# Two 16-head attentions on one core: steps taken in pairs, values gathered in bursts, projections in 32-column tiles

## The chip, the core and the metric

The kernel runs on one core of a Trainium2 chip. The core has a matrix engine (TensorE, PE in the profile, with its weight loads listed as PEld), a vector engine (DVE), a scalar engine (ACT), a general-purpose engine (POOL) and a queue that starts transfers (SP). PE reads its operands from the on-chip memory SBUF and writes results to the accumulation memory PSUM, which has 8 banks of 2 KB per partition; here a bank holds a 128 x 512 float32 tile. ACT and DVE read PSUM, POOL does not.

The metric is the device time of one execution in microseconds (us). Three runs of the kernel before took 1714.59, 1716.47 and 1717.76 us; the median is 1716.47.

## The reference

The input x is 8 batches of 512 tokens of 128 numbers. Four blocks follow each other, each of the form x = layernorm(x + block(x)):

1. attention with 16 heads of 8 numbers and a bias that falls with the distance of key and query (ALiBi);
2. a gated feed-forward whose operands are rounded to a 4-bit float grid in blocks of 16;
3. the same attention without the bias;
4. two layers of a windowed attention with 8 heads of 64 and a gated feed-forward.

The change concerns blocks 1 and 3 (called attention 1 and attention 2 here):

```python
qkv = (x @ W_qkv.T + b_qkv).reshape(B, S, 3, 16, 8)         # q, k, v: [B, 16, S, 8]
scores = einsum('bhqd,bhkd->bhqk', q, k) / sqrt(8)           # S = 512
probs = softmax(scores - slope[h] * |pos_q - pos_k|)         # the bias in attention 1 only
out = einsum('bhqk,bhkd->bhqd', probs, v) -> [B, S, 128]
y = out @ W_out.T + b_out
```

## The kernel before, in words

All work is float32, or float32 read in a mode that PE passes through once ("fp32r"). A plain float32 product is issued as two PE instructions, which is why the profile counts twice the products that the code names.

**Units and steps.** An attention runs over 32 units: 8 batches times 4 groups of 4 heads. The 4 heads of a unit are two pairs (`pp` = 0, 1); the two heads of a pair (`j` = 0, 1) lie in partitions 0 to 63 and 64 to 127 of the operands `q` and `k`, so that two products with half the rows of the array run at once. A unit has 8 steps in each of two passes, and the second pass of a unit runs 16 steps (`LAG`) after the first, beside the first pass of the unit two further on. One call of `step` does one step of both:

- first pass, called S below: two products write the scores of 128 queries against 512 keys into `s_ps` (two banks, of which there are two sets, pool `as`); DVE takes the maximum over the keys (`m`, a TENSOR_REDUCE from 128 x 1024);
- second pass, called T below: two products write the scores transposed, 128 keys against 512 queries, into two banks `t_ps`. One row of `q` holds minus the maximum, so these scores are already shifted. In attention 1 four small products (called C below, `corrected`) add the part of the bias inside a block. ACT takes the exponentials into two tiles `e` (pool of 11).

On PE the order of a step is S, T, C. On ACT it is exp, exp. After the step come the functions that are listed for it in `todo`.

**Values.** `values(u, blk, part)` adds one block of 128 keys for 256 of the 512 queries: 4 products, one for each head of the unit, with 32 output columns each (8 value columns, a column of ones for the denominator, the rest zero). They go to 4 column tiles of the array at once and accumulate in `av`, one PSUM bank of its own (pool `aav`). There is one such call in each step, so PE changes from the half-row tiling of S, T and C to the 32-column tiling and back in each step. After the eighth call ACT copies `av` to `avs` (128 x 512).

**Around it.** `divide` turns `avs` on PE (`o_ps`), and DVE divides by the denominators. `shift` turns the maxima on PE (`m_ps`), ACT copies them, POOL starts two transfers that put them into the row of `q`. Once a batch there are `begin_x` (turn x), `begin_qk` for n = 0 and 1, `begin_v`, `end_o` and `end_y`: each is a product or a turn on PE into a bank and a copy on ACT, or for `end_y` a sum and statistics on DVE. `begin_qk` hands its result on to POOL, which splits it in two parts, and to transfers through DRAM that lay out the operands (`load_qk`). The projections use the whole 128 x 128 array.

**Banks.** PSUM is divided into `as` (2 sets of 2 banks), `at` (3 banks in turn, for T and for every other use) and `aav` (1 bank). A tile that takes a bank waits until the last reader of the tile before it in this bank is done.

**Order.** PE, ACT, DVE and POOL instructions of these stages are held in program order, engine by engine; what sets the order is thus the order of the calls in the loop over steps and the step at which `later` lists a function. `plan` lists them: with z the step at which the second pass of the unit begins, values at z+3 to z+10, `divide` at z+12, `end_o` at z+15, `end_y` at z+18, and the work for a later batch at fixed steps of the batch.

**The other stages.** `ffn0` (block 2) lies between the attentions and uses the same banks; the first pass of attention 2 begins at its end. `ffn1` (block 4) follows; its weights `w1_s` and `w2_s` are loaded during attention 1 into SBUF that is held for the whole kernel.

In the profile, products of the attentions carry line 259, turns line 260, and ACT, DVE and POOL work of the attentions line 48 (the helper that keeps the program order). Line 644 is the same for `ffn1`, 472 for `ffn0`.

Of the kernel before, what the change touches and what calls it, by code (L numbers as in the profile page):

```python
# [18 lines left out]
P = 128  # L19
# [32 lines left out]
def body(ctx, tc, x, consts, rows, wa0, wa1, acols, bo, wf, wqkv, wo, w1, w2, cols, b2r, qs, ks, out):  # L52
# [16 lines left out]
    w1_s = outer.tile([P, 2, 2 * HID], F32, name="w1_s")  # L69
    w2_s = outer.tile([P, 2, 3, D], F32, name="w2_s")  # L70
# [36 lines left out]
    def load_weights():  # L107
        held(out=cst[:, C_MASK0:C_ROT], in_=consts[:, C_MASK0:C_ROT])
        held(out=wa[1], in_=wa1)
        held(out=wqkv_s, in_=wqkv.rearrange("l p f -> p l f"))  # L110
        held(out=wo_s, in_=wo.rearrange("l (c p) d -> p l c d", p=P))
        held(out=w1_s, in_=w1.rearrange("l p f -> p l f"))
        held(out=w2_s, in_=w2.rearrange("l (c p) d -> p l c d", p=P))
        held(out=cols_s, in_=cols)
# [87 lines left out]

    def operand_steps(li, qs_, ks_, va, mm, tr, bank, work, dram, qb):
# [9 lines left out]
        def begin_qk(b, h, n, start=nc.sync.dma_start):  # L213
            ps = bank("qk_ps")
            mm(ps, lhsT=w[:, n * P : (n + 1) * P], rhs=h["xT"], start=True, stop=True)
            t = work.tile([P, S], F32, tag=f"x{n}", name="x", bufs=1)
# [27 lines left out]
        def begin_v(b, h):  # L244
            ps = bank("v_ps").rearrange("p (c d) -> p c d", c=NT)
            for c in range(NT):
                mm(ps[:, c, :], lhsT=h["xT"][:, c * P : (c + 1) * P], rhs=w[:, W_V : W_V + P], start=True, stop=True)
# [5 lines left out]
    def attention(li, alibi, qs_, ks_, va, batch, late=None, spare=None, alone=0):  # L253
# [7 lines left out]
        with ExitStack() as st:  # L261
            pool = lambda name, bufs, **k: st.enter_context(tc.tile_pool(name=f"{name}{li}", bufs=bufs, **k))
            bank = lambda name: p_t.tile([P, S], F32, tag="t", name=name)
# [21 lines left out]
            def step(u, i, v, k):  # L285


                if u:
                    blk, pp = i // 2, i % 2
                    p, lo = 2 * u["g"] + pp, (i // 2) * P  # L290
                    q, kk = qs_[u["b"] % 2], ks_[u["b"] % 2]
                    both = p_s.tile([P, 2, S], F32, tag="s", name="s_ps")
                    ps = [both[:, j, :] for j in range(2)]
                    for j in range(2):
                        r = slice(64 * j, 64 * j + 63)
                        mm(
                            ps[j], lhsT=q[r, p, lo : lo + P], rhs=kk[r, p, :], start=True, stop=True,
                            skip_group_check=True,
                        )
                if v:  # L300
                    vp, vlo = 2 * v["g"] + k % 2, (k // 2) * P
                    q, kk = qs_[v["b"] % 2], ks_[v["b"] % 2]
                    ts = [bank("t_ps") for j in range(2)]
                    for j in range(2):
                        r = slice(64 * j, 64 * j + 64)
                        mm(
                            ts[j], lhsT=kk[r, vp, vlo : vlo + P], rhs=q[r, vp, :], start=True, stop=not alibi,
                            skip_group_check=True,
                        )
                if u:  # L310
                    if i == 0:
                        u["m"] = small.tile([P, 2, 2, NT], F32, tag="m", name="m")
                    dve.tensor_reduce(u["m"][:, :, pp, blk], both, AX.X, ALU.max)
                if v:
                    if alibi:
                        corrected(ts, vlo)
                    for j in range(2):
                        e = work.tile([P, S], F32, tag="e", name="e", bufs=11)
                        act_.activation(e, ts[j], AF.Exp, scale=float(SLOPES[2 * vp + j]) if alibi else 1.0)
                        v["e"].append(e)  # L320

            def shift(u):

                ps = bank("m_ps")[0:16, 0:P]
# [11 lines left out]
            def values(u, blk, part):  # L336
# [982 lines left out]
```

## Time and profile before

The profiled execution took 1715.33 us, of which the profile's span is 1713.6 us. The table gives what matters from the page and from stretches of the span; the granted clock of PE is 1.00 in the two attention stretches.

| stretch | span, us | PE busy | DVE busy | ACT busy |
|---|---|---|---|---|
| whole span | 1713.6 | 1601.4 | 1382.6 | 1257.3 |
| one batch of attention 1 | 53.3 (189.9 to 243.2) | 51.88 | 44.90 | 40.63 |
| one batch of attention 2 | 50.1 (733.3 to 783.4) | 49.24 | 42.87 | 39.90 |

The first S starts at 30 us, T of attention 1 runs from 54 to 472 us, T of attention 2 from 607 to 1005 us; `ffn1` fills the rest.

How to read it: a line of the timeline gives the start, the time from the first start to the last end, the engine, the line of the code, the operation with output and inputs, and how many instructions were merged; in brackets the idle time of the engine ahead of it and what ended that. The time of one product includes some 0.17 us in which the next ones already run, so the distance from start to start is what a product costs PE.

### The profile page before, as it was taken

To read this page: it belongs to the slowest core of one execution; us is meant where nothing else is said; L and a number is where in the kernel's file an instruction comes from. 1 tells how busy PE (TensorE), PEld (TensorE's weight loads), DVE (VectorE), ACT (ScalarE), POOL (GpSimd) and SP (SyncE) were. 2 spreads that over 40 slices of the span, in tenths; PEclk is the share of its full clock that TensorE was granted. 3 is DMA by queue.
4 is the path that set the end of the run, shared out by engine and by line. 5 is a ranking of instruction groups with operands and counts; after the bars stand their busy time and mean duration, and the time that the engine had idled before them with its cause. 6 is when DMAs were issued, how large, how long until landed. Compare 5 with 4: busy or idle time off the path is not lost.

```text
span 1713.6 us, 40048 instructions
## 1 busy us (share of the span) xinstructions
PE 1601.4 (93%) x15281; PEld 932.7 (54%) x15281; DVE 1382.6 (81%) x2220; ACT 1257.3 (73%) x2996; POOL 912.6 (53%) x974
## 2 busy tenths in 40 slices
PE   3999999999988799999999989999999999999995
PEld 1455555555556534444444446666666666666664
DVE  4788888889568888888888748888888888888863
ACT  0577777777745577787787757778888878888883
POOL 3323333232247732223232268888888888888872
PEclk7899999999999989999999989999999999999998
DMA  6626232230010352333231101111111111111110
GB/s 134 154 67 154 54 74 53 57 69 11 8 13 1 80 116 46 73 63 70 59 73 28 45 7 42 35 35 35 41 36 38 38 36 37 44 41 41 36 35 25
DMA packets 92801, 90.11 MB, mean 53 GB/s; under 512 B 45969, under 2 KB 58257, under 8 KB 92610
## 3 DMA queue, kind: packets, MB, share of 16 engines
q1 hardware_dynamic: 87280, 85.49, 23.2%
q8 instruction: 122, 2.00, 0.5%
q10 hardware_dynamic: 1234, 1.52, 0.3%
q0 software_dynamic: 4096, 0.54, 0.2%
q14 instruction: 69, 0.57, 0.1%
HBM read 41.82 MB, written 18.87 MB: 35 GB/s over the span
## 4 chain that ended last, share of the span: by engine, by line
PE 74%; DVE 10%; ACT 6%; POOL 4%; issue 3%; DMA 2%; SPq 0%; DVEq 0%; ACTq 0%; POOLq 0%
PE av L259 15%; PE s_ps L259 11%; PE t_ps L259 8%; PE y_ps L644 5%; PE sp L644 5%; PE o_ps L644 3%; PE t_ps L644 3%; PE v_ps L644 3%; PE p_ps L644 2%; ACT e L48 2%; PE q_ps L644 2%; PE k_ps L644 2%; PE gp L644 2%; DVE m L48 2%; PE ap L644 2%
## 5 line engine op out<-in xcount | busy, mean ns | idle before, releaser
L48 DVE TENSOR_REDUCE m<-s_ps 128x2 f32<-128x1024 f32 x512 | 618.7, 1223 | 124.9 <-PE s_ps L259 116.0
L48 ACT ACTIVATE e<-t_ps 128x512 f32<-128x512 f32 x1024 | 556.7, 597 | 149.8 <-PE t_ps L259 140.7
L259 PE MATMUL av<-e,va 128*32 128x256 f32 x4096 | 328.1, 393 | 14.0 <-ACT avs L48 14.0
L259 PE MATMUL s_ps<-k,q 63*128 63x512 f32 x1024 | 263.4, 509 | 25.0 <-DMA q<-far 16.9
L48 POOL DMA_DIRECT2D q<-mt x128 | 69.1, 544 | 342.9 <-ACT mt L48 342.9
L259 PE MATMUL t_ps<-q,k 64*128 64x512 f32 x1024 | 231.8, 410 | 1.4 <-ACT e L48 1.3
L644 ACT ACTIVATE pw<-sp,m,was_v 128x128 f32<-128x128 f32 x512 | 227.6, 479 | 1.5 <-DVE m L644 1.0
L259 PEld LDWEIGHTS s_ps<-k,q 63*128 63x128 f32 x1024 | 98.7, 188 | 235.1 <-issue 139.7
L644 POOL TENSOR_TENSOR was_v<-was_v 128x16 f32<-128x16 f32 x64 | 187.7, 2933 | 5.3
L259 PEld LDWEIGHTS t_ps<-q,k 64*128 64x128 f32 x1024 | 140.7, 187 | 29.2 <-ACT e L48 16.7
L259 PEld LDWEIGHTS av<-e,va 128*32 128x32 f32 x4096 | 81.5, 108 | 103.8 <-issue 58.9
L644 POOL TENSOR_TENSOR pw<-pw,den 128x1024 f32<-128x1024 f32 x64 | 121.3, 1895 | 9.3 <-DVE den L644 9.3
L644 ACT ACTIVATION_READ_ACCUMULATOR pw<-sp,m,was_v 128x1 f32 x512 | 115.6, 226 | 0.0
L644 DVE TENSOR_REDUCE m<-sp 128x4 f32<-128x512 f32 x128 | 82.2, 683 | 21.8 <-PE sp L644 20.1
L644 POOL TENSOR_TENSOR was_k<-was_k,was_q 128x512 f32<-128x512 f32 x64 | 88.0, 1376 | 6.1 <-DVE was_q L644 6.1
L644 ACT COPY v<-v_ps 128x512 f32<-128x512 f32 x64 | 37.8, 591 | 72.6 <-PE v_ps L644 72.6
L48 POOL CAST parts<-x 128x512 fp32r<-128x512 f32 x32 | 19.5, 609 | 131.0 <-ACT x L48 131.0
L644 PEld LDWEIGHTS t_ps<-cst,was_k 128*128 128x128 f32 x512 | 59.8, 142 | 43.1 <-issue 22.8
L644 DVE COPY pT<-p_ps 128x512 f32<-128x512 f32 x128 | 79.9, 665 | 0.5 <-PE p_ps L644 0.5
L644 PEld LDWEIGHTS p_ps<-cst,pw 128*128 128x128 f32 x512 | 59.8, 141 | 32.3 <-issue 27.5
L644 DVE TENSOR_REDUCE was_v<-was_k 128x16 f32<-128x1024 f32 x64 | 77.1, 1204 | 0.0
L644 PE MATMUL y_ps<-wo_s,oT 128*128 128x128 f32 x512 | 73.9, 288 | 0.0
(191 smaller groups left out, 3189.9 us busy)
## 6 DMA issues: line engine op xcount, KB each, us to landing
far<-parts SPq DMA_DIRECT2D x64, 256.0 KB
q<-far SPq DMA_DIRECT2D x256, 64.0 KB
k<-far SPq DMA_DIRECT2D x240, 64.0 KB
ve<-v SPq DMA_DIRECT2D x112, 128.0 KB
xn<-in_x SPq DMA_DIRECT2D x8, 256.0 KB
q<-mt POOLq DMA_DIRECT2D x128, 4.0 KB, 2.9
hn<-xs SPq DMA_DIRECT2D x16, 128.0 KB
hn<-xs SPq DMA_DIRECT2D x16, 112.0 KB
```

What stands on the lines that cost most here:

```text
L48: return lambda *a, **k: self.tc.keep_in_program_order(f(*a, **k))
L259: mm = lambda *a, **k: tc.keep_in_program_order(nc.tensor.matmul(*a, **k))
L644: kept = lambda f: lambda *a, **k: tc.keep_in_program_order(f(*a, **k))
```

## The change

What it does:

1. **Pairs of steps.** The loop runs over pairs of steps. In a pair PE gets S, T, C, S, T, C (`scores` and `weights`, each called twice), and after that the listed functions of both steps, `values` and `shift` first. The second pass of a unit takes the four key blocks of one pair of heads and then those of the other (before: both pairs for a block, then the next block). The step numbers in `plan` are halved.
2. **Values in a burst.** `values(u, pp, c)` takes both heads of a pair, all four key blocks and 256 queries, as 16 products of 128 columns on 4 column tiles (2 heads times 2 blocks of queries). It is called once in a pair of steps, four times in a unit. Its result is 128 x 128, goes to one of the T banks, and ACT copies it to a quarter of `avs` at once. There is no bank `aav` any more.
3. **Banks.** `at` has two tags, `t0` and `t1`, with 2 banks each. T of the first step of a pair takes both banks `t0`, T of the second both `t1`. `values` takes a `t0`, `shift` a `t1`; all other uses take `t1` and `t0` in turn in the attentions, and `t1` in `ffn0` (but for `ht_ps`, which takes `t0`).
4. **Projections in 32-column tiles.** `begin_qk`, `begin_v` and `end_y` issue each product as four with 32 stationary columns (`in_tiles`).
5. **Memory.** `e` has 16 tiles instead of 11. To make room, the two tiles `x` of `begin_qk` become one, and `w1_s` and `w2_s` are allocated and loaded when `ffn1` starts.
6. `divide` reads `avs` in its new order; `end_o` moves from z+15 to z+16; the steps of attention 2 that run at the end of `ffn0` are taken as pairs.

```diff
+    def in_tiles(mm, dst, lhsT, rhs):
+        for r in range(0, P, 32):
+            mm(dst[r : r + 32], lhsT=lhsT[:, r : r + 32], rhs=rhs, start=True, stop=True)
...
-            mm(ps, lhsT=w[:, n * P : (n + 1) * P], rhs=h["xT"], start=True, stop=True)
-            t = work.tile([P, S], F32, tag=f"x{n}", name="x", bufs=1)
+            in_tiles(mm, ps, w[:, n * P : (n + 1) * P], h["xT"])
+            t = work.tile([P, S], F32, tag="x", name="x", bufs=1)
...
-            bank = lambda name: p_t.tile([P, S], F32, tag="t", name=name)
+            turn = [0]
+            def bank(name, n=None):
+                if n is None:
+                    turn[0] ^= 1
+                    n = turn[0]
+                return p_t.tile([P, S], F32, tag=f"t{n}", name=name)
...
+            def weights(v, k):
+                pp, blk = divmod(k, NT)
...
+                ts = [bank("t_ps", blk % 2) for j in range(2)]
+                for j in range(2):
+                    r = slice(64 * j, 64 * j + 64)
+                    mm(
+                        ts[j], lhsT=kk[r, p, lo : lo + P], rhs=q[r, p, :], start=True, stop=not alibi,
+                        skip_group_check=True,
+                    )
+                if alibi:
+                    corrected(ts, lo)
+                for j in range(2):
+                    e = work.tile([P, S], F32, tag="e", name="e", bufs=16)
+                    act_.activation(e, ts[j], AF.Exp, scale=float(SLOPES[2 * p + j]) if alibi else 1.0)
+                    v["e"].append(e)
...
-                ps = bank("m_ps")[0:16, 0:P]
+                ps = bank("m_ps", 1)[0:16, 0:P]
...
+            def values(u, pp, c):
+                if pp == 0 and c == 0:
+                    u["avs"] = work.tile([P, NT, P], F32, tag="avs", name="avs")
+                av = bank("av", 0)[:, 0:P]
+                for blk in range(NT):
+                    for j in range(2):
+                        for f in range(2):
+                            r, at = 64 * f + 32 * j, S // 2 * f + P * c
+                            mm(
+                                av[r : r + 32], lhsT=va[u["b"] % 2][:, blk, 4 * u["g"] + 2 * pp + j, :],
+                                rhs=u["e"][8 * pp + 2 * blk + j][:, at : at + P], start=(blk == 0), stop=(blk == NT - 1),
+                                skip_group_check=True,
+                            )
+                act_.copy(u["avs"][:, 2 * pp + c, :], av)
...
-            later = lambda s, f, *a: todo.setdefault(s, []).append((f, a))
+            later = lambda s, f, *a: todo.setdefault(s // 2, []).append((f, a))
...
-                    for blk in range(NT):
-                        for part in range(2):
-                            later(z + 2 * blk + 3 + part, values, units[n], blk, part)
+                    for i in range(NT):
+                        later(z + 4 + 2 * i, values, units[n], *divmod(i, 2))
...
+            first = [values, shift]
+            for z in range((B * G * NU + LAG + 20) // 2):
...
+                n, i = divmod(2 * z, NU)
+                m, k = divmod(2 * z - LAG, NU)
+                for t in range(2):
+                    if n < B * G:
+                        scores(units[n], i + t)
+                    if 0 <= m < B * G:
+                        weights(units[m], k + t)
+                while z in todo:
+                    for f, a in sorted(todo.pop(z), key=lambda x: first.index(x[0]) if x[0] in first else len(first)):
+                        f(*a)
+                yield z
...
-        p_s, p_t, p_av = (
-            psum.enter_context(tc.tile_pool(name=n, bufs=k, space=PSUM)) for n, k in (("as", 2), ("at", 3), ("aav", 1))
-        )
+        p_s, p_t = (psum.enter_context(tc.tile_pool(name=n, bufs=2, space=PSUM)) for n in ("as", "at"))
```

## The prediction

> **What bounds the kernel now.** I read the busy shares of the page, then those of one batch of each attention, then the timeline of PE inside a batch, because a share says that PE is busy and only the distances from start to start say with what. In the batch stretches PE is busy 51.89 of 53.3 us (attention 1, A1 below) and 49.24 of 50.1 us (A2). DVE comes next.
>
> ```profile
> PE 1601.4 (93%) x15281; PEld 932.7 (54%) x15281; DVE 1382.6 (81%) x2220; ACT 1257.3 (73%) x2996; POOL 912.6 (53%) x974
> ```
>
> One step of A1 and one of A2 on PE (start, length, operation):
>
> ```profile
> 254.14 0.50 PE L259 MATMUL s_ps<-k,q 63*128 63x512 f32 x2
> 254.47 0.40 PE L259 MATMUL t_ps<-q,k 64*128 64x512 f32 x2
> 254.71 0.24 PE L259 MATMUL t_ps<-tri,sel 64*128 64x64 bf16 x4
> 254.88 0.64 PE L259 MATMUL av<-e,va 128*32 128x256 f32 x8
> 255.45 0.51 PE L259 MATMUL s_ps<-k,q 63*128 63x512 f32 x2
> ...
> 793.31 0.50 PE L259 MATMUL s_ps<-k,q 63*128 63x512 f32 x2
> 793.64 0.39 PE L259 MATMUL t_ps<-q,k 64*128 64x512 f32 x2
> 793.97 0.64 PE L259 MATMUL av<-e,va 128*32 128x256 f32 x8
> 794.53 0.50 PE L259 MATMUL s_ps<-k,q 63*128 63x512 f32 x2
> ```
>
> A step costs 1.31 us in A1: S to T 0.33, T to C 0.24, C to values 0.17, values to the next S 0.57. In A2 it costs 1.23: 0.33, 0.33, 0.57. T and S stream the same 512 columns, but T to C (no change of tiling) takes 0.23 to 0.24 and T to values (a change) 0.33: a change of tiling costs about 0.1, and the S behind it pays 0.1 again, since its weights are not loaded ahead.
>
> A unit is 8 steps and some more: `o_ps` starts at 250.34 and at 262.36 (12.02 us) in A1, at 789.69 and 800.83 (11.14 us) in A2. In A1, 8 x 1.31 = 10.48, `o_ps` 0.58, `m_ps` 0.20, and two waits: 0.39 of the first values for the copy `avs`, 0.30 of a T for an exponential. In A2 the same two are 0.27 and 0.2.
>
> ```profile
> 261.07 0.64 PE L259 MATMUL av<-e,va 128*32 128x256 f32 x8 [0.39 <-ACT avs L48]
> ```
>
> A batch is three such units and a heavy one that carries the operands and the end of a batch: 53.3 - 36.05 = 17.25 us in A1, 50.1 - 33.4 = 16.7 in A2.
>
> **Part 1, PE alone: a gain.** Per pair of steps, two changes of tiling instead of four. The burst is 16 products, 32 instructions of 128 columns on four column tiles. The nearest row is block 4's window scores, 32 instructions of 128 columns on four tiles, a change of tiling on either side:
>
> ```profile
> 1310.70 1.10 PE L644 MATMUL sp<-kT,qT 64*64 64x128 f32 x32
> 1311.73 0.44 PE L644 MATMUL hT<-cst,was_v 128*128 128x128 f32 x2
> ```
>
> 1.03 us to the next start; I take it. Two calls before cost 2 x 0.57 = 1.14. A pair in A1: S to T 0.33, to C 0.24, to S 0.17, to T 0.23 (weights now loaded ahead; 0.33 if not), to C 0.24, to values 0.17, to the next S 1.03: 2.41, against 2.62. In A2: 0.33 + 0.23 + 0.23 + 0.33 + 1.03 = 2.15 against 2.46. The two waits go as well, since values get a bank that the first exponential has freed long ago. PE alone would make units of 4 x 2.41 + 0.78 = 10.42 (A1) and 4 x 2.15 + 0.78 = 9.38 (A2); in A2 DVE would stop it at 8 x 1.24 + 0.25 + 0.29 = 10.46 (four maxima back to back take 4.97).
>
> The page "TensorEngine Tiling" of the Trainium skill, Performance Considerations, speaks against the finer burst: each matmul has some 60 cycles of overhead, and a tiling factor should not be taken from a dimension that is already small. The row above shows no such cost: 32 in 1.03 us are 32 ns each, which the streaming of four tiles fills. By the rule, as an estimate at the 2.4 GHz of the page "TensorE: Matmul & The Clock Gate" (Part 1), 16 more instructions a pair would cost 16 x 25 ns = 0.4 us, and some 250 pairs 100 us. The row decides.
>
> **Part 2, the new wait: a ring through the banks.** T of the first step of a pair takes both banks `t0`. The burst at the end of the pair before used one of them, and its copy stands on ACT behind all four exponentials of that pair. So the second T waits for this copy, and S, T, C and the burst stand behind that T on PE, and the next exponentials behind them. In A1:
>
> ```profile
> 302.48 1.10 ACT L48 ACTIVATE e<-t_ps 128x512 f32<-128x512 f32 x2
> ...
> 303.14 0.18 PEld L259 LDWEIGHTS t_ps<-q,k 64*128 64x128 f32 x1 [0.15 <-ACT e L48]
> ...
> 303.79 0.60 ACT L48 ACTIVATE e<-t_ps 128x512 f32<-128x512 f32 x1 [0.21 <-PE t_ps L259]
> ```
>
> This T waited for an exponential: it ended at 303.08, the load began 0.06 later, the next exponential 0.65 after the load. Two exponentials take 1.10 and one 0.60, so they start 0.49 to 0.50 apart. The copy, 128 x 128, has its row in the weights' copy:
>
> ```profile
> L48 ACT COPY wd<-w_ps 128x128 f32<-128x128 f32 x2 | 0.4, 270 | 0.0
> ```
>
> The ring: 0.06 + 0.65 + 4 x 0.49 + 0.27 = 2.94 us a pair. That is more than PE's 2.41, so `o_ps` (0.58) and `m_ps` (0.20) hide in it, and a unit is 4 x 2.94 = 11.76. Four exponentials in A2 took 2.26, 0.55 apart; whether they waited for PE there I can't tell, so 0.55 is the other end: ring 3.18. I take 0.49, seen where the second was surely ready.
>
> In A2 the first T need not wait, and its exponential covers the wait of the second; the ring closes over two pairs. From S: first exponential at 0.33 + 0.44 = 0.77 (T at 830.04, exponential at 830.48), copy done at 0.77 + 1.96 + 0.27 = 3.00, load of the waiting T at 3.06, then 0.34 to S, 0.23 to T, 0.33 to the burst, 1.03: the S of the pair after next at 4.99. Two pairs before: 4.92. The extras add to it: 2 x 4.99 + 0.78 = 10.76 a unit against 11.14.
>
> **Part 3, other users of the banks.** They alternate between `t1` and `t0`; counting the calls, in A1 two of four `o_ps`, `v`, `ot` and `y` of a batch fall on `t0`, in A2 two `o_ps`, `xt` and both `qk`. The second T of the next pair then waits for their reader. `o_ps` on `t0` in A1: the burst ends 2.16 after the T load, the turn's 0.66 and DVE's 0.25 and 0.29 with gaps end at 3.45: 0.55 late, twice a batch. On `t1` it waits for the first exponential there: 0.17. In A2 the pair has slack for it. A1, three units: 3 x 11.76 + 1.1 + 0.17 = 36.55 (before 36.05).
>
> Heavy unit, extras from distances of starts: `v` 1.09, `xt` 0.58, `ot` 0.59, `qk` 1.06 and 1.05, `y` 1.09. These pairs are bound by PE. A1: 2.41 + 0.58 + 1.09 + 0.15; 2.41 + 0.58 + 0.58 (T waits for the copy of `v`); 2.41 + 0.20 + 0.59 + 1.06; 2.41 + 1.09 + 1.05: 16.6 (before 17.25). A2: 2.5 + 0.58 + 1.09; 2.15 + 0.58; 2.15 + 1.85 + 0.6 (copy of `xt`, 0.59 long); 2.15 + 2.14 + 0.78 (copy of the first `qk`, 0.78 long): 16.6 (before 16.7). The 32-column projections stream the same columns and spare a change of tiling behind a burst, 0.1 at most a time; I count nothing.
>
> **Small edits.** One tile `x`: at the start the second copy (13.72) must await POOL (13.55 + 1.26): +0.8 us on the way to the first S. Later the two are a pair apart. The 16 steps of A1 with T alone: 1.30 each before, now the ring: +0.9. `ffn0`: its four banks are used as before, the finer projections add changes of tiling: +0.5. Loading `w1_s` and `w2_s` late: two issues on SP (0.6 to 2.8 us each at 141 us), ahead of it nothing, behind it `hn` loads and the first `ve` copy (1020.41); their first reader is at 1038.9, some 25 us after A2's end. Nothing; without that cover the 1.07 MB would cost some 10 us, at 100 to 150 GB/s as seen early. `shift` now issues behind the burst: its ACT copy (0.24), two POOL issues (1.1) and landing (2.9) need 4.3 us of the three pairs (7.4) left. ACT's copies of the burst, 4 x 0.27 instead of 0.59 a unit, are in the ring. DVE has the same work. Five more tiles `e` keep the values, used up to four pairs late, off the exponentials' way.
>
> **Sum.** A1: 8 x (+0.5 - 0.65) = -1.2. A2: 8 x (3 x -0.38 - 0.1) = -9.9. Small edits +2.2. Together -8.9 us on the profiled execution's 1715.33 (span 1713.6): 1706.4. The median lies 1.1 above that execution: 1707.5, say 1707.
>
> **Rivals.** *PE decides* (0.13): the copy comes early enough. Units of 10.42 and 10.46: 24 x 1.6 + 24 x 0.68 = 55, the heavy ones 11: 1650. For it: PE is busy 97%. Against: each link of the ring is a row.
>
> *The ring is longer* (0.30), slower than before. Exponentials 0.55 apart give 3.18 in A1 (24 x 4 pairs and 8: +25) and 5.23 for two pairs in A2 (48 x 0.24 = +11.5): 1743. It passes the old time once the exponentials are over 0.51 apart, or any link 0.07 longer. For it: the row of four in 2.26, and that each wait I left out adds to a ring and not to an idle engine.
>
> *Nothing left* (0.12): waits on the `t0` users eat the rest, 1716.
>
> **How the numbers follow.** 0.2% is 3.4 us, about what a measurement tells from no change. The likeliest case (0.45) is 1697 to 1717: 0.30 faster, 0.08 same, 0.07 slower. PE decides: faster. Longer ring: slower. Nothing left: 0.03, 0.05, 0.04. Faster 0.46, same 0.13, slower 0.41. The range goes from 1680, about halfway to the fast rival, to 1746, the long ring and 3 us, and leaves out some 0.16.
>
> **What would show it.** Right: starts of the first S of two pairs 2.9 to 3.0 us apart in A1, alternating about 2.2 and 2.8 in A2; T's second load released by the copy; changes of tiling halved; bursts of 1.03; no wait of values for `avs`; PE's share lower than 97% in A1. Wrong: bursts over 1.1, exponentials over 0.51 apart, DVE without idle time in A2, or waits at `ffn1`'s start for `w_s`.

## The result, and the profile after

The changed kernel takes 1720.89 us (median of 12 runs, 1719.23 to 1723.20), the kernel before 1717.44 us beside it (12 runs). The ratio is 1.0021, with a 95% interval of 1.0012 to 1.0030: slower by 3.4 us, where 9 us faster was forecast. The profiled execution took 1719.23 us, of which the span is 1717.5.

The row of engines on the page of the kernel after (busy time, share of the span, instructions), and two groups of its PE weight loads (busy time, mean ns | idle time before them, and what ended most of it). After the change products of the attentions carry line 260, turns line 261 and `ffn1` line 656.

```profile
PE 1583.5 (92%) x20336; PEld 1065.4 (62%) x20337; DVE 1370.1 (80%) x2220; ACT 1249.8 (73%) x3188; POOL 912.6 (53%) x974
...
L260 PEld LDWEIGHTS av<-e,va 128*32 128x32 f32 x8192 | 209.5, 110 | 85.2 <-ACT e L48 77.3
...
L260 PEld LDWEIGHTS t_ps<-q,k 64*128 64x128 f32 x1024 | 162.8, 188 | 75.3 <-ACT avs L48 28.5
```

PE is busy 18 us less than before (1601.4) and yet the span is 4 us longer: PE does less and waits more. The waits have two names, T for the copy of a burst (28.5 us, foreseen; on the page of the kernel before, all idle time ahead of T's loads was 29.2) and the burst for an exponential (77.3 us, not foreseen).

One ordinary pair of attention 1, on ACT and then on the weight loads of PE (start, length, operation):

```profile
314.57 2.06 ACT L48 ACTIVATE e<-t_ps 128x512 f32<-128x512 f32 x4 [0.55 <-PE t_ps L260]
316.50 0.30 ACT L48 COPY avs<-av 128x128 f32<-128x128 f32 x1
317.50 2.06 ACT L48 ACTIVATE e<-t_ps 128x512 f32<-128x512 f32 x4 [0.70 <-PE t_ps L260]
```

```profile
315.22 0.81 PEld L260 LDWEIGHTS av<-e,va 128*32 128x32 f32 x32 [0.23 <-ACT e L48]
316.23 0.19 PEld L260 LDWEIGHTS s_ps<-k,q 63*128 63x128 f32 x2 [0.20 <-issue]
316.34 0.19 PEld L260 LDWEIGHTS t_ps<-q,k 64*128 64x128 f32 x1
316.85 0.18 PEld L260 LDWEIGHTS t_ps<-q,k 64*128 64x128 f32 x1 [0.32 <-ACT avs L48]
```

This is the ring of the prediction: exponentials from 314.57, the copy behind them at 316.50, the second load of T released by it at 316.85, the next first exponential at 317.50. One round, from first exponential to first exponential, is 2.93 us. The burst costs 1.01 (315.22 to 316.23). The burst's own wait is also here: it begins 0.65 after the first exponential has begun, since it takes that exponential's bank.

Where the 3.9 us between the two profiled executions lie, cut at starts of PE instructions of attentions 1 and 2 (A1 and A2 below):

| stretch | before | after | difference | forecast |
|---|---|---|---|---|
| start to first T | 53.68 | 53.76 | +0.1 | +0.8 |
| A1, first T to last S | 395.21 | 400.06 | +4.85 | -1.2 |
| A1, last S to the first gate product of `ffn0` | 26.25 | 28.56 | +2.3 | +0.9 |
| `ffn0`, to the first T of A2 | 131.79 | 131.71 | -0.1 | +0.5 |
| A2, first T to last T | 398.55 | 390.10 | -8.45 | -9.9 |
| last T to the first window score of `ffn1` | 10.14 | 12.68 | +2.5 | 0 |
| rest | 697.97 | 700.62 | +2.65 | 0 |

Attention 2 and the small edits came near the forecast. Attention 1 lost 6 us against it, the end of attention 2 some 2.5. Of the change the last row holds only the late loads of `w1_s` and `w2_s`, and these do not show in it: e4 and e8 below, which load them there too, have 697.6 and 697.9 us in this row. But in the stretch from 1660 to 1700 us the granted clock was 0.91 in this execution and 1.00 in that of before. Such dips lie at different places in different executions (see the end), so that one row of a single execution can be off by 3 to 4 us. The A1 row is touched too: from 56.2 to 62.8 us the clock was 0.50 in the execution of before and 1.00 in the other.

The steady batches, in the middle of each attention and at a clock of 1.00, are free of this. One of A1 took 53.3 us before and 54.0 after, 0.7 more where 0.15 less was forecast; one of A2 50.05 and 49.15, 0.9 less where 1.24 less was forecast.

### The profile page after: what moved, and what is told of

It reads as the page before. It is cut to its first block, busy times and chain, and to the rows that moved or that the text cites. A ratio compares the mean times of both kernels' runs of the same rounds, so it can differ in the third digit from the quotient of the medians.

```text
span 1717.5 us, 50434 instructions
## 1 busy us (share of the span) xinstructions
PE 1583.5 (92%) x20336; PEld 1065.4 (62%) x20337; DVE 1370.1 (80%) x2220; ACT 1249.8 (73%) x3188; POOL 912.6 (53%) x974
## 4 chain that ended last, share of the span: by engine, by line
PE 65%; DVE 14%; ACT 9%; POOL 5%; issue 3%; DMA 2%; SPq 1%; ACTq 0%; DVEq 0%; POOLq 0%
PE av L260 12%; PE t_ps L260 7%; PE s_ps L260 7%; ACT e L48 6%; PE y_ps L656 5%; DVE m L48 5%; PE sp L656 4%; PE o_ps L656 3%; PE t_ps L656 3%; PE v_ps L656 3%; PE p_ps L656 2%; PE q_ps L656 2%; PE k_ps L656 2%; PE gp L656 2%; PE ap L656 2%
## 5 line engine op out<-in xcount | busy, mean ns | idle before, releaser
L48 DVE TENSOR_REDUCE m<-s_ps 128x2 f32<-128x1024 f32 x512 | 600.9, 1218 | 106.9 <-PE s_ps L260 102.3
L48 ACT ACTIVATE e<-t_ps 128x512 f32<-128x512 f32 x1024 | 532.7, 603 | 142.9 <-PE t_ps L260 140.1
L260 PE MATMUL s_ps<-k,q 63*128 63x512 f32 x1024 | 294.4, 487 | 32.2 <-DMA q<-far 18.7
L260 PE MATMUL t_ps<-q,k 64*128 64x512 f32 x1024 | 298.7, 420 | 10.0 <-ACT x L48 3.3
L260 PE MATMUL av<-e,va 128*32 128x128 f32 x8192 | 277.7, 277 | 24.0 <-ACT e L48 13.4
L260 PEld LDWEIGHTS av<-e,va 128*32 128x32 f32 x8192 | 209.5, 110 | 85.2 <-ACT e L48 77.3
L260 PEld LDWEIGHTS t_ps<-q,k 64*128 64x128 f32 x1024 | 162.8, 188 | 75.3 <-ACT avs L48 28.5
L260 PEld LDWEIGHTS s_ps<-k,q 63*128 63x128 f32 x1024 | 121.1, 189 | 108.5 <-issue 55.9
L260 PE MATMUL t_ps<-tri,sel 64*128 64x64 bf16 x1024 | 97.2, 195 | 0.0
L48 ACT COPY avs<-av 128x128 f32<-128x128 f32 x256 | 75.4, 295 | 4.2 <-PE av L260 4.2
```

Source lines behind the costliest of these rows:

```text
L48: return lambda *a, **k: self.tc.keep_in_program_order(f(*a, **k))
L260: mm = lambda *a, **k: tc.keep_in_program_order(nc.tensor.matmul(*a, **k))
```

## The experiments

All times are medians; the ratio is to runs of the kernel before on the same chip in the same series (1716.9 to 1717.5 us).

| run | time, us | ratio, 95% interval |
|---|---|---|
| changed kernel | 1720.89 | 1.0021 (1.0012 to 1.0030) |
| e1 four banks in turn | 1676.20 | 0.9768 (0.9755 to 0.9781) |
| e2 in turn, burst between the steps | 1681.46 | 0.9801 (0.9788 to 0.9813) |
| e3 copies twice | 1746.32 | 1.0172 (1.0159 to 1.0185) |
| e4 plain projections | 1718.39 | 1.0010 (1.0001 to 1.0020) |
| e5 T ahead of S | 1743.31 | 1.0153 (1.0139 to 1.0166) |
| e6 in turn, T ahead of S | 1675.70 | 0.9752 (0.9739 to 0.9765) |
| e7 in turn, T ahead, burst between | 1674.61 | 0.9751 (0.9738 to 0.9764) |
| e8 no tokens, changed | 1715.53 | 0.9987 (0.9977 to 0.9998) |
| e9 no tokens, before | 1715.40 | 0.9989 (0.9980 to 0.9998) |
| e10 a bank for the burst alone | 1782.15 | 1.0381 (1.0367 to 1.0395) |
| e11 the same, burst between | 1772.67 | 1.0322 (1.0307 to 1.0336) |
| e12 in turn, plain projections | 1678.41 | 0.9765 (0.9752 to 0.9779) |
| e13 other uses on t1 only | 1708.18 | 0.9940 (0.9927 to 0.9954) |

### The ring: e1 and e3

The first question is whether the ring of banks is what paces the changed kernel. e1 opens it, e3 makes its copy longer.

```diff
-                return p_t.tile([P, S], F32, tag=f"t{n}", name=name)
+                return p_t.tile([P, S], F32, tag="t", name=name)
...
-        p_s, p_t = (... tc.tile_pool(name=n, bufs=2, ...) for n in ("as", "at"))
+        p_s, p_t = (... tc.tile_pool(name=n, bufs=k, ...) for n, k in (("as", 2), ("at", 4)))
```

> Edit: the four T banks carry one name and are taken in turn by T, values and all other uses, so the copy of the burst now holds back the second bank of the pair's second T, not of its first; the burst still takes the bank of the pair's first exponential. Theory 'ring' (copy behind four exponentials -> second half of the first T, 2.92 us a pair): the first T waits for exponentials of the pair before, long done; the wait of t_ps for avs (28.5 us) goes to under 5 us, ordinary units of attention 1 fall from 12.4 to about 10.6 (the chain first exponential 0.44 after T, burst 0.65 after it, 1.01 to the next S, 0.33 to T is 2.43, plus 0.2 a pair for o_ps and m_ps), of attention 2 from 10.95 to about 10.5 (the vector engine's 10.46): 24 x 1.8 + 24 x 0.45 = 54 less, about 1667. Rival 'vector engine': both maxima of a pair come within 0.6 us, so S waits for DVE whatever the banks do; then attention 1 stays within 0.5 us a unit and the time is over 1700.

```diff
-                act_.copy(u["avs"][:, 2 * pp + c, :], av)
+                for _ in range(2):
+                    act_.copy(u["avs"][:, 2 * pp + c, :], av)
```

> Edit: each copy of a burst to avs is issued twice (1024 instead of 512 a launch in all, 256 more in each attention). Theory 'ring': in attention 1 every ordinary pair is bound by the copy, which gets 0.16 to 0.27 longer: 128 ordinary and up to 120 heavy pairs, of which I count the 96 ordinary and a third of the heavy: 130 x 0.2 = +26 in attention 1; in attention 2 the ring closes over two pairs, so half of that, +13: about 1760. Rival 'bank wait and vector engine' (the ring is slack in most pairs): ACT is busy 73% and takes them in its idle time: under +10, below 1731.

e1 took 1676.20 us, 45 less than the changed kernel. The same two groups on its page:

```profile
L260 PEld LDWEIGHTS av<-e,va 128*32 128x32 f32 x8192 | 210.9, 111 | 90.5 <-ACT e L48 85.8
...
L260 PEld LDWEIGHTS t_ps<-q,k 64*128 64x128 f32 x1024 | 121.5, 189 | 18.0 <-PE s_ps L260 3.7
```

T's wait for `avs` is gone. A steady batch of A1 fell from 54.0 to 51.7 us, one of A2 from 49.2 to 47.0. The burst's wait for an exponential did not fall, it rose from 77.3 to 85.8. So the larger of the two waits on the page cost the changed kernel next to nothing: the ring was longer than it and covered it. "Ring" holds; its size in A2 was right (ordinary units 10.53, expected about 10.5), in A1 it was too hopeful (12.0, expected 10.6), for a reason that the next section shows.

In e3 a launch has 512 copies instead of 256 (the counts in the expectation are twice too high). It took 1746.32, 25 more than the changed kernel and between the theories. The rows say where:

```profile
265.31 2.06 ACT L48 ACTIVATE e<-t_ps 128x512 f32<-128x512 f32 x4 [0.49 <-PE t_ps L260]
267.24 0.60 ACT L48 COPY avs<-av 128x128 f32<-128x128 f32 x2
268.48 2.06 ACT L48 ACTIVATE e<-t_ps 128x512 f32<-128x512 f32 x4 [0.65 <-PE t_ps L260]
```

A copy more is 0.30, and a round 3.17 instead of 2.93. Over a batch the pairs gave 1.7 (A1) and 1.5 us (A2), where 16 copies of 0.30 are 4.8: that is what a third of the pairs would give if the ring bound them. In the others heavy work, DVE or a reader of a bank ends last; these were not taken apart. In A2 two pairs went from 5.21 to 5.50: one copy in two pairs, which is the ring over two pairs as forecast.

### The loss in attention 1: e8 and e9

Once in each of the first seven batches, attention 1 also rounds tokens for `ffn0`. It is work of DVE, ACT and POOL, and the prediction did not speak of it. DVE, ACT and the S that waits for DVE, from the timeline of the changed kernel (`qy` and `qm` are the rounding's tiles):

```profile
249.81 0.19 PEld L260 LDWEIGHTS s_ps<-k,q 63*128 63x128 f32 x2 [0.20 <-issue]
...
250.11 0.63 ACT L48 ACTIVATE qm<-qy 128x512 f32<-128x512 f32 x1
...
250.78 0.43 DVE L48 TENSOR_SCALAR qm<-qm 128x512 f32<-128x512 f32 x1 [0.50 <-ACT qm L48]
...
250.91 2.06 ACT L48 ACTIVATE e<-t_ps 128x512 f32<-128x512 f32 x4 [0.17 <-PE t_ps L260]
...
251.31 0.69 DVE L48 TENSOR_TENSOR qy<-qy,qm 128x512 f32<-128x512 f32 x1
...
251.92 2.35 DVE L48 TENSOR_REDUCE m<-s_ps 128x2 f32<-128x1024 f32 x2
...
253.19 0.18 PEld L260 LDWEIGHTS s_ps<-k,q 63*128 63x128 f32 x2 [0.20 <-DVE m L48]
...
254.32 0.19 PEld L260 LDWEIGHTS s_ps<-k,q 63*128 63x128 f32 x2 [0.45 <-DVE m L48]
```

The maxima of the first pair begin 2.11 us after its S (249.81 to 251.92), where a pair without the rounding shows 0.55. Both S of a pair are meant to go 0.6 us apart and take both sets of `s_ps`; with DVE late, the second S of the next pair starts 1.13 behind the first (253.19, 254.32), and T, C and the burst stand behind it. ACT's own part of the rounding (0.63) is not what holds the pair: it lies in the gap ahead of the exponentials, which then still wait 0.17 for T. But DVE waits 0.50 for it. Both runs leave the rounding out:

```diff
-                later(done(b), tokens, b)
+                pass
```

> Edit: the changed kernel without rounding the feed-forward's input tokens of the first seven batches to their grid (left out of attention 1; the output differs). That is work of DVE, ACT and POOL beside attention 1 only. Theory 'late vector engine' (in the pairs that carry the rounding both maxima of a pair start late and hold back the second S): four pairs a batch go from about 3.35 to 2.93, seven batches x 4 x 0.4 = 11 less: about 1710. Rival 'ring and bank wait' (DVE's lateness is hidden in the ring): under 3 less, 1718 to 1721.

> Edit: the kernel before, likewise without rounding the input tokens of the first seven batches (left out of attention 1; the output differs). In the changed kernel this took 0.94 us off a batch of attention 1 (54.05 to 53.11) and 5.4 off the time. Theory 'the change made DVE's lateness cost': single scores a step leave DVE time to catch up, so the kernel before loses nothing to the rounding and stays within 1.5 us (a batch within 0.2 of 53.29). Rival 'the rounding costs both': a batch falls to about 52.4 and the time by 5 to 6.

The changed kernel fell by 5.4 us (1720.89 to 1715.53), about half of what its theory said and more than the rival allowed. The kernel before fell by 2.1 (1717.53 to 1715.40), a little over the 1.5 of its theory, but its steady batch of A1 hardly moved (53.3 to 53.2). Without the rounding the two ratios are 0.9987 and 0.9989: no difference is left. The stage says the same. A1 from the first T to the last S took 400.06 us after and 395.21 before; without rounding it took 394.89 and 394.88 (in e9, as in the kernel before, the stage begins with a dip of the clock, from 53.3 to 63.3 us; in e8 it does not). A steady batch of the changed kernel fell from 54.02 to 53.13, which is what the prediction had worked out from the ring (36.55 + 16.6 = 53.15; e8 has 36.4 and 16.7). In such a batch of e8, eight of the twelve rounds of the ordinary units are 2.92 or 2.93 long. The timeline of e8 in one of the pairs that carry the rounding in the changed kernel:

```profile
293.91 0.19 PEld L260 LDWEIGHTS s_ps<-k,q 63*128 63x128 f32 x2 [0.20 <-DVE m L48]
...
294.48 2.36 DVE L48 TENSOR_REDUCE m<-s_ps 128x2 f32<-128x1024 f32 x2 [0.67 <-PE s_ps L260]
...
294.57 0.19 PEld L260 LDWEIGHTS s_ps<-k,q 63*128 63x128 f32 x1
```

Here DVE waits for PE (0.67), the maxima begin 0.57 after S, and the second S follows at 0.66. The five pairs around the rounding took 15.0 us in e8 and 16.1 in the changed kernel. The units of a steady batch of A1, from S to S, show where the rounding sits; e1 and e13 (next section) have the rounding and other banks:

| unit | changed kernel | e8 | e13 | e1 |
|---|---|---|---|---|
| first ordinary | 12.49 | 12.03 | 12.49 | 12.49 |
| second ordinary | 12.39 | 11.91 | 12.39 | 12.39 |
| third ordinary | 12.46 | 12.46 | 11.93 | 11.05 |
| heavy | 16.70 | 16.71 | 16.68 | 15.82 |

The first two ordinary units carry the rounding. There three kernels with different banks take the same time; with the rounding out it falls by 0.46 and 0.48. The rows above are from a second unit. In the first one DVE's work is also longer than before, by one instruction of the rounding, `sc`. The changed kernel:

```profile
297.85 1.28 POOL L48 TENSOR_TENSOR parts<-x,parts 128x512 fp32r<-128x512 f32 x1
298.13 1.04 DVE L48 TENSOR_SCALAR sc<-sc 128x32 f32<-128x32 f32 x1
```

The same instruction on the page of the kernel before (busy time, mean ns):

```profile
L48 DVE TENSOR_SCALAR sc<-sc 128x32 f32<-128x32 f32 x8 | 1.6, 203 | 0.3
```

In the steady batches of the kernel before it takes 0.18 us, and POOL is idle at that time. In the changed kernel it ends 0.04 after POOL has split the result of `begin_qk`, which now runs beside it, and takes 1.04 us.

So the loss in A1 against the forecast is the rounding. How much of it is the longer `sc` and how much the late maxima was not tried apart. That the kernel before hides the rounding because it asks for one maximum in a step of 1.31 us, where the reduction takes 1.2, fits its rows but was not tried apart either.

### Other uses of the burst's bank: e13

```diff
                 if n is None:
-                    turn[0] ^= 1
-                    n = turn[0]
+                    n = 1
```

> Edit: the changed kernel, but all uses of a bank other than T and the burst take t1 (before: t1 and t0 in turn), one line. Theory 'o_ps on t0' (in attention 2 the burst's wait sets the pair at 2.43 to 2.50, so a second T that waits for DVE's o on t0 adds 0.22, twice a batch; in attention 1 it adds 0.55 against 0.17 on t1, twice a batch): attention 2 0.4 a batch less (49.15 to 48.7), attention 1 0.4 to 0.8 less (54.05 to 53.4): 8 to 10 less than the changed kernel, 1711 to 1713, if the once-a-batch products, which then follow each other through t1, lose nothing. Rival 'the heavy unit loses as much' (y, qk, v and xt all wait on t1 for the third and fourth exponential, up to 0.5 each, five a batch): 1720 to 1730. Rival 'the ring covers o_ps anyway': 1719 to 1722.

1708.18, 12.7 us less than the changed kernel, from one line. A pair of A2 with `o_ps`, the changed kernel first, then e13 (weight loads of PE):

```profile
842.98 0.42 PEld L261 LDWEIGHTS o_ps<-cst,avs 128*128 128x128 f32 x4 [0.20 <-ACT e L48]
...
843.68 0.19 PEld L260 LDWEIGHTS t_ps<-q,k 64*128 64x128 f32 x1
844.38 0.18 PEld L260 LDWEIGHTS t_ps<-q,k 64*128 64x128 f32 x1 [0.51 <-PE t_ps L260]
```

```profile
842.60 0.42 PEld L261 LDWEIGHTS o_ps<-cst,avs 128*128 128x128 f32 x4 [0.20 <-ACT e L48]
...
843.30 0.19 PEld L260 LDWEIGHTS t_ps<-q,k 64*128 64x128 f32 x2
```

In the changed kernel `o_ps` sits on `t0`, and the second load of T stands 0.70 us behind the first; in e13 both loads go at once. (The bracket of that load names PE's own T as what came last. That it is the bank of `o_ps` is shown by e13, where only the banks differ; DVE was done with `o_ps` at 844.26, 0.12 ahead of this load.) A steady batch of A2 fell from 49.2 to 48.4 us, of A1 from 54.0 to 53.5. In A1 the pairs behind an `o_ps` on `t0` fell, from 3.12 to 2.56 in the third unit and from 3.15 to 2.50 in the first; but there the next pair rose from 3.36 to 4.03, since its S waits 1.08 for DVE, which is at the rounding, and the unit stays at 12.49. The gain is larger than the 8 to 10 expected; the theory that the ring covers `o_ps` falls.

### The division of the banks: e10 and e11

Was the bank plan of the change a mistake as such? These two put back the division of before: three banks in turn, one for the burst.

```diff
-        p_s, p_t = (... bufs=2 ... for n in ("as", "at"))
+        p_s, p_t, p_av = (... bufs=k ... for n, k in (("as", 2), ("at", 3), ("aav", 1)))
...
-                return p_t.tile([P, S], F32, tag=f"t{n}", name=name)
+                return p_t.tile([P, S], F32, tag="t", name=name)
...
-                av = bank("av", 0)[:, 0:P]
+                av = p_av.tile([P, S], F32, tag="av", name="av")[:, 0:P]
```

> Edit: the changed kernel with the banks divided as before the change: three banks in turn for T and the other uses, one bank for the burst alone. The burst waits for no exponential, only for its own last copy; the second half of the second T waits for this pair's first exponential, which ended some 0.1 to 0.2 before. Theory 'the division of the banks took the gain': the pairs and bursts then give what PE alone should, about 10.5 a unit in both: 1660 to 1675, level with the banks in turn. Rival 'three banks are too few for T': waits of t_ps for e eat half of it: 1685 to 1700.

> Edit: as the run before, with the burst between the two steps of its pair, one pair later (18 tiles e, one avs, two o). The second T then comes 1.75 after the first and waits for nothing; the burst neither. Theory 'waits of PE are what is left': 10 less than the run with the bank alone, 1655 to 1665. Rival 'DVE and ACT pace the batch' (the runs with four banks in turn all ended at 1675 to 1681): 1675 again.

Both theories of e10 fell: 1782.15, 61 us slower than the changed kernel. Both of e11 fell as well: 1772.67. T's loads in two pairs of e10:

```profile
272.87 0.18 PEld L260 LDWEIGHTS t_ps<-q,k 64*128 64x128 f32 x1 [0.64 <-ACT e L48]
...
275.93 0.18 PEld L260 LDWEIGHTS t_ps<-q,k 64*128 64x128 f32 x1 [0.63 <-ACT e L48]
```

The fourth half of T in a pair needs the bank of the pair's first exponential and waits 0.63 for it; a pair takes 3.06 (272.87 to 275.93). With three banks two T this close together wait for a bank; with four in turn (e1) these waits are gone. The change was right to give the fourth bank to T; what costs is that names tie the burst to the bank of the next first T.

### The order on PE: e5, e2, e6 and e7

e5 keeps the banks of the change and puts T and C ahead of S in each step, meaning to take away the burst's wait.

```diff
-                    if n < B * G:
-                        scores(units[n], i + t)
                     if 0 <= m < B * G:
                         weights(units[m], k + t)
+                    if n < B * G:
+                        scores(units[n], i + t)
```

> Edit: the changed kernel with its own banks t0 and t1, but in each step the shifted scores and their bias come ahead of the scores (T C S instead of S T C). The first exponential of a pair then starts 0.33 us earlier against the burst, and the burst should find its bank free; the copy of the burst still holds back the second half of the next first T. Theory 'missed wait' (the ring alone was foreseen rightly; the burst's wait for the first exponential turned o_ps and m_ps from covered into added time): the 77 us of av behind e go to under 20, ordinary pairs without other work stay at 2.93 us, twelve ordinary pairs of a batch of attention 1 go from 37.3 to about 36.5, together 5 to 10 less than the changed kernel: 1711 to 1716. Rival 'vector engine': scores of a pair are as close as before, so nothing changes: 1719 to 1723. Rival 'ring shorter': if the chain over the first exponential was what closed the ring, pairs fall to 2.6 and the time to about 1690.

It took 1743.31, slower by 22 us, which no theory gave. PE's weight loads in it:

```profile
276.22 0.18 PEld L260 LDWEIGHTS t_ps<-q,k 64*128 64x128 f32 x1 [0.30 <-ACT avs L48]
...
277.70 0.16 PEld L260 LDWEIGHTS av<-e,va 128*32 128x32 f32 x8 [0.24 <-ACT e L48]
```

The burst still waits. The exponential of the pair needs its C, C stands behind both halves of T, and the second half waits for `avs`: moved ahead, T moves its wait along. The ring itself is as long as it was (first exponentials at 273.94, 276.87 and 279.81). What the order took away is S between the burst and the waiting T, 0.33 us of cover, which shows in the pairs with other work. That this is all of the 22 us was not shown.

In e2 the banks go in turn and the burst stands between the two steps of its pair; e6 is e1 with the order of e5; e7 has both.

```diff
                     if 0 <= m < B * G:
                         weights(units[m], k + t)
+                    if t == 0:
+                        for f, a in [x for x in todo.get(z, []) if x[0] is values]:
+                            f(*a)
...
-                        later(z + 4 + 2 * i, values, units[n], *divmod(i, 2))
+                        later(z + 6 + 2 * i, values, units[n], *divmod(i, 2))
```

> Edit: as in the run with the banks in turn, and the burst stands between the two steps of its pair (S T C, burst, S T C), one pair later, so that it takes a bank freed a pair ago and its copy stands on ACT behind two exponentials; 18 tiles e, paid for by one avs and two o. Same number of changes of tiling. Theory 'ring and bank wait': PE pair 2.41 + 0.2 of other work, no waits of av for e, DVE at 2.6 a pair level with it: ordinary units 10.6 and 10.5, the time 1655 to 1675, at or below the run with the banks in turn by 0 to 15 us, since the wait of the burst (90 us in rows av after e) is gone and the maxima come evenly. Rival 'vector engine by total': it stays at DVE's 44.9 us a batch at best and nothing is gained over the banks in turn. Rival 'PE alone' : if the burst's wait cost nothing because PE had slack, the two runs agree within 3 us.

> Edit: banks in turn (as in the run before of that name) and T C S in each step. Theory 'missed wait': without the ring the burst's wait for the first exponential (85.8 us in the run with the banks in turn) is what is left on PE in attention 1; pairs without other work go from 2.56 to 2.41-2.45, and o_ps and m_ps add 0.2 a pair as there: 12 ordinary pairs 1.4 less, 8 batches 11, attention 2 about 5: 1660 to 1664. Rival 'vector engine': S of a pair stay 0.6 apart, S waits for m (66 us with the banks in turn) grow by what the burst's wait loses: 1672 to 1680.

> Edit: banks in turn, T C S, and the burst between the two steps (T C S, burst, T C S; 18 tiles e, one avs, two o). Scores come 1.2 us apart, the burst's bank is that of an exponential of the pair before, the copy stands behind two exponentials. Theory 'waits': PE pair 2.41 and 2.15, DVE level: 16 pairs and extras 47.2 to 49 us a batch of attention 1 (51.7 with the banks in turn) and 46 of attention 2 (47.0): 25 less than with the banks in turn, about 1650. Rival 'something else paces' (DVE's own total, or ACT): no better than the better of the two runs before it, 1676.

1681.46, 1675.70 and 1674.61: with the ring open, three orders on PE end within 2 us of e1 or above it. (e2 lies 5 above; why was not shown.) The theories that promised a gain over e1 fell; the rivals "vector engine" of e6 and "something else paces" of e7 hold by the time. The wait of the burst fell (85.8 in e1, 62.7 in e6, 48.2 in e2, 39.2 in e7) and the time did not follow. What paces instead is not the same everywhere. In A2 of e1 it is still the burst's wait: a pair without other work takes 2.43 us there, which is the chain that the expectation of e1 adds up, and an ordinary unit 10.5. In e6 and e7 these units took 10.2 to 10.4; DVE's maxima, two in 2.36 us, and `divide` (0.25 + 0.29) need 4 x 2.36 + 0.54 = 9.98. So DVE is near. In A1 the two units with the rounding took 11.9 to 13.0 us in all four kernels and the third 11.0 to 11.2, so the units that carry the rounding are the long ones there too; what paces the third stays open. e7 and e6 are the fastest runs, 2.5% under the kernel before; e1 is level with them and one small edit from the change.

### The projections: e4 and e12

```diff
-            in_tiles(mm, ps, w[:, n * P : (n + 1) * P], h["xT"])
+            mm(ps, lhsT=w[:, n * P : (n + 1) * P], rhs=h["xT"], start=True, stop=True)
```

(and likewise in `begin_v` and `end_y`)

> Edit: the projections are whole 128 x 128 products again. Theory 'counted at nothing': within 3 us of the changed kernel (1718 to 1724). Rival 'finer projections cost': each begin_qk, begin_v and end_y has 12 more products pairs of instructions; if these cost 25 ns each, 3 x 24 instructions x 25 ns a batch and attention is 1.8, 16 batches 29 us less without them: about 1692. Rival 'they spare changes of tiling behind a burst': +0.1 x 4 x 16 = +6 without them.

> Edit: four banks in turn, order S T C, and the projections as whole products. Theory 'the finer projections cost 2 us' (1718.4 against 1720.9 in the changed kernel): 1673 to 1675. Rival 'noise of that size': 1676 to 1677.

1718.39 against 1720.89 in the changed kernel, and 1678.41 against 1676.20 with the banks in turn: 2.5 less, 2.2 more. The intervals overlap in both cases. "Counted at nothing" holds to some 3 us; the rival of 29 us is out.

## Why the prediction was wrong, step by step

**Part 1, PE alone: right.** The burst cost 1.01 us to the next start (1.03 taken). The page "TensorEngine Tiling" of the Trainium skill, Instruction Overhead, puts some 60 cycles on every matmul; here 32 instructions pass in 1.01 us, 32 ns each, so the price that I worked out from that rule, 0.4 us more in a pair, is not seen. The sentence "The two waits go as well, since values get a bank that the first exponential has freed long ago" failed: the burst found that bank busy in most pairs (77.3 us in all). It cost next to nothing, because the ring was longer: with the ring open (e1) the wait grew and the time fell by 45 us.

**Part 2, the ring: right.** 2.93 against 2.94 in A1; in A2 two pairs took 5.21 with a `m_ps` of 0.20 in them, against 4.99 and the extras on top. Exponentials stood 0.48 to 0.49 apart (0.49 taken), the copy took 0.30 (0.27). One sign of it failed: rounds of A2 do not alternate between 2.2 and 2.8, they take 2.43 and, with the `m_ps` taken off, some 2.57. The burst's wait, which the prediction had left out, lengthens the short round, and the sum over two hides it.

**Part 3, other users: half right.** In A1 the `t0` users were priced, in A2 the step "In A2 the pair has slack for it" failed: the pair behind an `o_ps` on `t0` was 0.22 longer than that behind one on `t1` (2.71 against 2.49), and the once-a-batch products showed up too. A2 gained 0.9 us in a steady batch instead of 1.24. e13 prices all uses of `t0` at 12.7 us.

**"DVE has the same work": the step that decided.** The prediction put DVE at nothing by this sentence, and the sentence failed twice. It takes the sum for the time: the change issues both S of a pair within 0.6 us, and in the pairs where the rounding of tokens holds DVE up, the second S waits. And the sum is not the same where it matters: once a batch `sc` takes 1.04 us instead of 0.18, beside POOL. With the rounding out, a steady batch of A1 falls by 0.9 us in the changed kernel and by 0.1 in the kernel before, the medians by 5.4 and 2.1, the profiled stage by 5.2 and 0.3. That leaves 3 us of the medians and 5 of the stage to this step: of the 12 us between forecast and result the largest piece that was found.

**Small edits: near, but for one that was missed.** Start and `ffn0` cost nothing (+1.3 counted), the tail of A1 2.3 (0.9 counted). Not counted: the end of A2. There three bursts stand in a row behind the last T, and the first one waits for an exponential that ACT reaches late, after 1.50 us in which ACT waits for DVE's work of `ffn1` (ACT, then PE):

```profile
1005.34 0.60 ACT L656 ACTIVATE was_k<-s_ps 128x512 f32<-128x512 f32 x1 [1.50 <-DVE was_q L656]
...
1006.47 4.42 PE L260 MATMUL av<-e,va 128*32 128x128 f32 x96 [1.82 <-ACT e L48]
```

From the last T to the first window score it took 12.5 to 13.0 us in the changed kernel and in e1, e3 to e6, e8, e12 and e13, all with the burst at the end of its pair on a bank of T; it took 10.1 in the kernel before and 8.8 in e9. The clock has a share in these times: it was 0.50 from 1006.5 to 1009.7 in the changed kernel, where the three bursts took 4.42 us instead of 2.83 in e2, and 0.50 from 1011.9 on in the kernel before, but 1.00 in e9. It took 10.2 with a bank for the burst alone (e10), 14.4 in e11, and 9.1 with the burst between the steps on a bank of T (e2, e7). In e10, e2 and e7 the last T itself waits 1.82, 1.49 and 1.48 for the exponential, ahead of this stretch, so their shorter times do not show that the wait is gone. No run changed this place alone.

**The rivals.** "PE decides" was the fast one, 1650: with the ring open the time is 1675, and DVE's rounding in A1 and the burst's wait in A2 come ahead of PE. "The ring is longer" did not happen. "Nothing left", 1716, is nearest in time, by a mechanism it did not name in full: waits on `t0` and DVE.

**What stays open.** The stages that hold the change's work add up to +1.25 us of the profiled difference, the rest row to +2.65 with its dip of the clock, while the medians differ by 3.45 (2.1 to 5.2). One or two us are not accounted for.

## What to carry to other kernels

When work is bunched into bursts, go through every engine that serves it and ask what each must now deliver in the short stretch, not only over the batch: here DVE's maxima were as many as before, and the new order exposed 3 to 5 us of DVE's other work. Look as well at what now runs beside what: one short instruction of DVE took 1.04 us instead of 0.18 beside one of POOL. A buffer that one name ties to a late reader makes a ring; give the buffers in turn to whoever comes next and the late reader falls on the request that can wait longest (45 us here, for one name instead of two). A long wait on the profile is no price as long as something longer covers it: 77 us of it went on in the faster kernel and grew.

The page "Perfetto Trace Analysis" of the Trainium skill, Optimizing Tensor Performance, says that independent groups of matmuls should rotate through different PSUM banks, so that taking one out overlaps the next. This case agrees: four banks in turn took 1676 us, the same four under two names 1721.

## What the runs showed of the hardware that was not expected

The two halves of a product that use half the rows of the array each run on apart. Where the second half of T waited for `avs` (316.85 in the rows above, against 316.34 for the first load), S, T and C behind it were loaded one half at a time (S at 316.90 and 317.23, T at 317.01 and 317.34), to the next burst.

DVE's short `sc` does not end before an instruction of POOL that runs beside it: 1.04 us in the changed kernel, 0.60 in e2 and 0.57 in e6, where it starts later against POOL, each time 0.03 to 0.04 behind the end of POOL's, and 0.18 in the kernel before, where POOL is idle. DVE's maxima are not lengthened by the same POOL instruction: in e8 it runs from 294.17 to 295.45, and the two maxima from 294.48 take 2.36 as elsewhere.

The granted clock falls below 1.00 in stretches that differ from one execution to the next: from 1660 to 1700 us it was 0.91 in the changed kernel and 1.00 in the kernel before; from 980 to 1000 us 0.74 in e8 and 1.00 in the kernel before. Taken in narrow windows these are short stretches at 0.50: from 1672.1 to 1675.3 and from 1689.1 to 1692.3 in the changed kernel, with 1.00 between, and from 981.3 to 991.3 in e8. They are not confined to the end: the changed kernel has 0.50 from 491.1 to 494.3 and from 610.5 to 620.5 too. In e8 a burst inside the stretch from 981.3 took 1.93 us instead of 1.08:

```profile
977.43 1.08 PE L260 MATMUL av<-e,va 128*32 128x128 f32 x32 [0.51 <-ACT e L48]
...
986.92 1.93 PE L260 MATMUL av<-e,va 128*32 128x128 f32 x32
```

In that execution A2 took 394.4 us instead of 390.1, though e8 changes nothing in A2. A difference of a few us in one stage of one execution is therefore no evidence before the clock of that stretch has been read.
